# Variances of two batches computed in earlier gaps of VectorE, router scores between two transposed tiles, ten dummy products instead of eight, and eight instead of four shared tiles added ahead of the final sums

## The chip, the cores and the metric

The kernel runs on one core of a Trainium2 chip. A core has TensorE (PE: matrix products into PSUM; the weight loads before them are shown as PEld), VectorE (DVE), ScalarE (ACT), GpSimd (POOL) and SyncE (SP), which here only issues DMAs. Each engine takes its instructions strictly in the order in which they were written and waits, where it must, for marks that the other engines and the DMAs set. The metric is the time of one execution on the device, in microseconds (us).

## The reference

Four batches of 512 tokens of width 512 go through two gated residual steps. `x` is (4, 512, 512); the context is (4, 64, 128), 64 keys for each batch.

```python
def xattn(q, latent_kv, Wq, Wkv_expand, Wout):          # 16 heads of 32
    qp = q @ Wq.T
    k, v = jnp.split(latent_kv @ Wkv_expand.T, 2, axis=-1)
    scores = jnp.einsum('bhqd,bhkd->bhqk', qh, kh) / sqrt(32)
    scores = jnp.where(tril, scores, finfo.min)
    out = jnp.einsum('bhqk,bhkd->bhqd', softmax(scores), vh)
    return out @ Wout.T

def ffn(x, gate_w, w1, w2, w3, ws1, ws2, ws3):          # 8 experts, inner width 256
    scores = softmax(xf @ gate_w.T)
    weights, idx = top_k(scores, 2)
    eo = silu(xf @ w1.T) * (xf @ w3.T) @ w2.T           # per expert
    y = sum over the two chosen experts of weight * eo
    z = silu(xf @ ws1.T) * (xf @ ws3.T) @ ws2.T         # shared expert
    return y + z

x = x + tanh(g_xattn) * xattn(layernorm(x), ctx, ...)
x = x + tanh(g_ffn)   * ffn(layernorm(x), ...)
```

The layer norm has no weights: each row minus its mean, divided by sqrt(variance + 1e-5). Everything is float32.

## The kernel before

Tokens lie in tiles of 128 rows, four to a batch, sixteen in all. The kernel has three stages, and in each the order of the work on PE, DVE, ACT and POOL is the order of the Python statements (a "manual schedule"); no planner moves anything on these four engines. SP's order is by hand in the stage of the experts only.

**Attention** (`attention()`). The loop `for b in range(B)` handles the attention of batch b, and beside it the end of batch b-1 ("last"): its output projection (`project_out`, PE tile `pd`, L360), the residual sum into `xs` (L364), the second norm, and the router. For one batch:

- `score_products` (PE tile `psc`, L299) makes the scores of two of the four tiles; it is called twice.
- `largest` (DVE, L314) finds each row's maximum straight from `psc`; `exponentials` subtracts it (DVE, L319) and takes exp on ACT (L320); `softmax` sums (DVE, L325), inverts (L327) and lets POOL multiply (L328). The four tiles are p0 to p3.
- `transpose_p` turns one such tile on PE (eight transposes, tile `pp`, L335), and ACT copies them out (`prt`, L338, two copies a tile).
- `attend` multiplies with the values (PE tile `po`, L349; ACT copies `at`, L354).
- For batch b+1 the rows are turned (`turn`: PE `pt`, L190; ACT copies `xt`, L191) and projected (`project_q`: PE `pq`, L285, one chunk of 128 columns in 3.5 us; ACT copies `qt`, L289).
- `first_rows(b + 2)` norms the rows of batch b+2: `moments` (four pairs of DVE L148 and L149), `deviation` (DVE L155, square root on ACT L157, five small DVE operations L161 to L167) and `normalize` (four of DVE L177).
- For batch b-1, `second_rows_of` norms its rows (DVE L177), `turn` turns them into `x2t`, `gate` (PE `pg`, L372; ACT copy `parts`, L377) and `gate_sum` (PE `pl`, L383) make the router's scores. `choose` finds the two best experts by a chain of some thirty small DVE operations (L395 to L438) around one exp on ACT (L418); `route` and `scatter` then give each row its place (PE L445 and L448, DVE L454 to L459), and POOL writes each row twice into a table in DRAM (`xg_d`, indirect DMA, L464, eight for one batch).

exp, square root and SiLU need different function tables on ACT; a table load (ACT_TABLE_LOAD) stands ahead of the first use after another table. `table_of(AF.Exp)` is a tiny exp (L625) that brings that load forward.

The products in PSUM share a ring of four buffers (`ps_mm`: tiles `pp`, `pt`, `pq`, `pg`, `pl`, `po`, `pd`, `pz` and the shared expert's `ph`); the fifth product must wait until the first has been copied out. The last batch has no next batch to project (`more` is false), so two halves of the shared expert (`shared_pair`, PE L583, ACT SiLU L600, DVE product L601, which the code calls `gated`) fill the gaps.

Before the first score, PE makes eight dummy products `pw` (L630). From 25 us on SP writes zeros over `xg_d` (L246) and over the result table `y_d` (L250), some 41 MB, at the rate of the DMA queue; POOL's first indirect write may not go before the last zeros of `xg_d` have landed.

**Experts.** `last_routing` ends batch 3; then a loop over 32 to 39 tiles of 128 gathered rows: PE `ph` (L868) and `py` (L895), POOL adds each result row into `y_d` (L902).

**The end.** The shared expert's second product (`shared_down`, PE tile `pz`, L929, 1.72 us a tile) is still wanted for each of the sixteen tiles, and is multiplied by a gate and added on DVE. For the first `ahead` tiles (`shared_onto_attended`, L938) the sum goes onto `xs`, which needs nothing from the experts. For the others it goes onto `yk` (L1018), the experts' sums, two tiles to a buffer, which eight DMAs read back from `y_d` (L992), and only after DVE has added `xs` (`add_attended`, L999). `store` (SP, L1002) writes a finished tile out.

Of the kernel before, what the change touches and what calls it, by code (L numbers as in the profile page):

```python
# [15 lines left out]
AF = mybir.ActivationFunctionType  # L16
# [4 lines left out]
B, S, D = 4, 512, 512  # L21
# [3 lines left out]
DC = D // P  # L25
QT = S // P
# [21 lines left out]
def gated_cross_attention_moe(  # L48
# [157 lines left out]
    with ExitStack() as attn:  # L206
# [268 lines left out]
        def new_qt():  # L475
            return a2.tile([P, DC, S], F32, tag="qt", name="qt")

        def first_rows(b):
            for t in range(QT):
                moments(b, mv1[b], t)  # L480
            deviation(mv1[b], rstd1[b])()
            xn = [a4.tile([P, D], F32, tag="xn", name="xn") for t in range(QT)]
            for t in range(QT):
                normalize(xn[t], b, t, mv1[b], rstd1[b])
            return xn
# [132 lines left out]
        def attention():  # L618
            xn = [a4.tile([P, D], F32, tag="xn", name="xn") for t in range(QT)]
            nc.gpsimd.tensor_copy(ctx_sb[:, :, 1, :], ctx_sb[:, :, 0, :])  # L620
            small_one = small.tile([P, 1], F32, tag="one", name="one", bufs=1)

            def table_of(function):

                nc.scalar.activation(small_one, ones[:, 0:1], function)  # L625


            pw = ps_mm.tile([P, P], F32, tag="mm", name="pw")
            for _ in range(8):
                nc.tensor.matmul(pw, ident, ident, start=True, stop=True)  # L630
            table_of(AF.Sqrt)
            xt, qt = new_xt(), new_qt()
            mv, rstd = mv1[0], rstd1[0]
            for t in range(2):
                moments(0, mv, t)
            rest = deviation(mv, rstd, range(0, 2))
            for half in range(2):
                project_keys(half)
            rest()
            for t in range(2):  # L640
                normalize(xn[t], 0, t, mv, rstd)
            for t in range(2):
                transpose_rows(xn[t], t, xt)
            for t in range(2, QT):
                moments(0, mv, t)
            rest = deviation(mv, rstd, range(2, QT))
            project_q(xt, qt, range(DC), slice(0, 2 * P))
            rest()
            for t in range(2, QT):
                normalize(xn[t], 0, t, mv, rstd)  # L650
            for t in range(2, QT):
                transpose_rows(xn[t], t, xt)
            project_values(0)
            xn = first_rows(1)
            project_q(xt, qt, range(DC), slice(2 * P, S))
            for f, i in counts:
                nc.vector.tensor_copy(f, i)
            at = qt_next = None
            parts = iter([(c, f) for c in range(B - 1) for f in range(FC)])
            for b in range(B):  # L660
                more, last = b + 1 < B, b - 1
                prt = ab.tile([P, NPAIR, S], F32, tag="prt", name="prt")
                psc = score_products(b, 0, qt)
                if b > 1:
                    places, scatter = route(last - 1, *chosen)
                if more:
                    xt, qt_next = new_xt(), new_qt()
                    turn(xn, xt)
                if not b:
                    project_values(1)  # L670
                p0 = exponentials(*largest(psc, 0))
                p1 = exponentials(*largest(psc, 1))
                if not b:
                    nc.scalar.activation(tg_x, tg_x, AF.Tanh)
                    nc.scalar.activation(tg_f, tg_f, AF.Tanh)
                if b > 1:
                    places()
                softmax(p0)
                if b:
                    mv, rstd = new_stats()  # L680
                    project_out(last, at, 0)
                    moments(last, mv, 0)
                softmax(p1)
                if b > 1:
                    for t in range(QT):
                        scatter(t)
                if b:
                    for t in range(1, QT):
                        project_out(last, at, t)
                        moments(last, mv, t)  # L690
                    rest = deviation(mv, rstd)
                    if more:
                        table_of(AF.Exp)
                else:
                    project_q(xt, qt_next, range(2))
                psc = score_products(b, 1, qt)
                if not b:
                    transpose_p(p0, prt, 0)
                    transpose_p(p1, prt, 1)
                if b and more:  # L700
                    project_q(xt, qt_next, range(1))
                elif b:
                    gated, _ = shared_pair(*next(parts))
                    table_of(AF.Exp)
                p2 = largest(psc, 2)
                if b:
                    rest()
                p2 = exponentials(*p2)
                p3 = exponentials(*largest(psc, 3))
                if b:  # L710
                    if more:
                        project_q(xt, qt_next, range(1, 2))
                    else:
                        gated()
                    xn2 = new_rows(last)
                    second_rows_of(xn2, last, mv, rstd)
                softmax(p2)
                softmax(p3)
                if b:
                    transpose_p(p0, prt, 0)  # L720
                    transpose_p(p1, prt, 1)
                    turn(xn2, x2t[last])
                if more:
                    project_q(xt, qt_next, range(2, DC))
                    if b:
                        scored = gate(last)
                else:
                    gated, scored = shared_pair(*next(parts), lambda: gate(last))
                    gated()
                if b + 2 < B:  # L730
                    xn = first_rows(b + 2)
                if not more:
                    scores = gate_sum(scored)
                transpose_p(p2, prt, 2)
                if not b:
                    project_values(2)
                transpose_p(p3, prt, 3)
                if not b:
                    project_values(3)
                    table_of(AF.Exp)  # L740
                if b and more:
                    scores = gate_sum(scored)
                attended = []

                def attend_now():
                    attended.append(attend(b, prt))

                if b:
                    chosen = (xn2, *choose(last, scores, attend_now))
                else:  # L750
                    attend_now()
                (at,) = attended
                qt = qt_next

            scoring.close()
            attn.close()
            return at, chosen, parts
# [230 lines left out]
    with tc.manual_schedule(engines={ET.PE, ET.DVE, ET.Activation}):  # L988
        yk = []
        for i in range(0, NT, 2):  # L990
            yk.append(yp.tile([P, 2, D], F32, tag="yk", name="yk"))
            nc.sync.dma_start(  # L992
                out=yk[-1], in_=y_rows[ts(i // 2, 2 * P), :].rearrange("(t p) d -> p t d", p=P)
            )
        def add_attended(i):

            b, t = divmod(i, QT)
            y = yk[i // 2]
            nc.vector.tensor_tensor(y, y, xs[b][:, t : t + 2, :], ALU.add)  # L999

        def store(i, columns=slice(0, D)):
            nc.sync.dma_start(out=out[ts(i, P), columns], in_=yk[i // 2][:, i % 2, columns])  # L1002


        ahead = QT
        for i in range(1, ahead):
            shared_onto_attended(i)
        for i in range(0, ahead, 2):
            add_attended(i)
            store(i)  # L1010
            store(i + 1)
        for i in range(ahead, NT):
            if i % 2 == 0:
                add_attended(i)
            for c in range(0, D, D if i < NT - 1 else YH):
                columns = slice(c, D if i < NT - 1 else c + YH)
                y = yk[i // 2][:, i % 2, columns]
                nc.vector.scalar_tensor_tensor(  # L1018
                    y, shared_down(i, columns), tg_f, y, ALU.mult, ALU.add
                )  # L1020
                store(i, columns)
# [52 lines left out]
```

## Time and profile before

| | us |
|---|---|
| median of 3 runs (471.78 to 473.58) | 472.6 |
| the profiled execution | 474.84 |
| its span, first to last instruction | 473.1 |
| PE busy in the span | 456.8 |
| DVE, ACT, POOL busy | 250.1, 130.6, 179.2 |

All times of the trace are counted from the start of the span. The attention stage lasts until about 190 us, the routing of the last batch to 235, the experts from 246 to 435, the end from there on. In the trace's lines the first number is the start, the second the busy time, `x4` the number of instructions merged into the line, and the bracket at the end how long the engine had stood idle and what ended that.

### The profile page before, as it was taken

To read this page: it belongs to the slowest core of one execution; us is meant where nothing else is said; L and a number is where in the kernel's file an instruction comes from. 1 tells how busy PE (TensorE), PEld (TensorE's weight loads), DVE (VectorE), ACT (ScalarE), POOL (GpSimd) and SP (SyncE) were. 2 spreads that over 40 slices of the span, in tenths; PEclk is the share of its full clock that TensorE was granted. 3 is DMA by queue.
4 is the path that set the end of the run, shared out by engine and by line. 5 is a ranking of instruction groups with operands and counts; after the bars stand their busy time and mean duration, and the time that the engine had idled before them with its cause. 6 is when DMAs were issued, how large, how long until landed. Compare 5 with 4: busy or idle time off the path is not lost.

```text
span 473.1 us, 6677 instructions
## 1 busy us (share of the span) xinstructions
PE 456.8 (97%) x1970; PEld 234.1 (49%) x1970; DVE 250.1 (53%) x600; ACT 130.6 (28%) x244; POOL 179.2 (38%) x188
## 2 busy tenths in 40 slices
PE   7999999999999989999999999999999999999876
PEld 6775455564556555445444444444444444444333
DVE  3557788769937983557323333343333433333385
ACT  2345752573454274423011111111111111110000
POOL 3003312301480474342500656556565565655200
PEclk9999999999999999999999999999999999999979
DMA  7989999999964040899745766665666656544594
GB/s 274 310 308 384 386 386 385 387 385 386 400 259 87 1 183 2 321 417 418 283 84 123 120 106 104 102 97 90 103 98 104 99 91 102 70 52 57 155 395 184
DMA packets 70785, 98.13 MB, mean 207 GB/s; under 512 B 11728, under 2 KB 40144, under 8 KB 69584
## 3 DMA queue, kind: packets, MB, share of 16 engines
q1 hardware_dynamic: 58096, 80.01, 50.0%
q0 software_dynamic: 12352, 17.57, 20.8%
q8 instruction: 19, 0.31, 0.3%
q14 instruction: 30, 0.25, 0.2%
q10 hardware_dynamic: 288, 0.00, 0.0%
HBM read 34.84 MB, written 62.71 MB: 206 GB/s over the span
## 4 chain that ended last, share of the span: by engine, by line
PE 79%; DVE 10%; DMA 7%; ACT 2%; issue 1%; SPq 1%; another core or an unknown queue 0%; DVEq 0%
PE ph L868 23%; PE py L895 11%; PE pq L285 10%; PE pd L360 9%; PE ph L609 6%; DMA y_d<-y,meta 5%; PE pz L929 4%; PE pt L190 3%; PE ph L583 3%; PE psc L299 2%; DVE mx L314 2%; PE early L583 1%; PE pg L887 1%; PE pp L335 1%; DMA yk<-y_d 1%; DVE pr L319 1%
## 5 line engine op out<-in xcount | busy, mean ns | idle before, releaser
L902 POOL DMA_INDIRECT y_d<-y,meta x68 | 105.6, 1553 | 103.1 <-DVE y L899 60.9
L868 PE MATMUL ph<-w_all,xgt 128*128 x272 | 122.6, 593 | 0.1
L868 PEld LDWEIGHTS ph<-w_all,xgt 128*128 128x128 f32 x272 | 49.1, 190 | 49.6 <-issue 49.5
L328 POOL TENSOR_TENSOR pr<-pr,rs 128x1024 f32<-128x1024 f32 x16 | 30.2, 1902 | 111.9 <-DVE rs L327 91.2
L895 PE MATMUL py<-w_all,gt 128*128 x136 | 63.9, 592 | 0.0
L879 DVE SCALAR_TENSOR_TENSOR g<-sl,w,ph 128x256 f32<-128x256 f32 x34 | 16.3, 481 | 87.0 <-ACT sl L877 84.6
L285 PE MATMUL pq<-xt,wq_sb 128*128 128x512 f32 (+1 forms) x160 | 56.9, 511 | 0.7 <-ACT xt L191 0.7
L360 PE MATMUL pd<-wo_sb,at 128*128 128x512 f32 x128 | 56.1, 595 | 0.0
L877 ACT ACTIVATE sl<-ph 128x256 f32<-128x256 f32 x34 | 13.1, 384 | 109.0 <-PE ph L868 58.1
L895 PEld LDWEIGHTS py<-w_all,gt 128*128 128x128 f32 x136 | 25.8, 190 | 32.5 <-issue 32.5
L285 PEld LDWEIGHTS pq<-xt,wq_sb 128*128 128x128 f32 x160 | 29.7, 190 | 24.3 <-issue 20.1
L360 PEld LDWEIGHTS pd<-wo_sb,at 128*128 128x128 f32 x128 | 23.9, 190 | 29.1 <-issue 27.3
L899 DVE COPY y<-py 128x512 f32<-128x512 f32 x34 | 23.5, 692 | 27.8 <-PE py L895 27.8
L929 PE MATMUL pz<-sh,gs_sb 128*128 128x512 f32 (+1 forms) x68 | 31.0, 615 | 5.5 <-DVE yk L1018 4.6
L609 PE MATMUL ph<-x2t,sh 128*128 128x512 f32 x64 | 28.6, 596 | 0.0
L889 ACT COPY gt<-pg 128x256 f32<-128x256 f32 x34 | 12.7, 372 | 53.1 <-PE pg L887 53.1
L148 DVE BATCH_NORM_STATS2 st<-x 128x6 f32<-128x512 f32 x32 | 21.8, 680 | 7.3 <-DMA x<-in_x_dram 6.8
L929 PEld LDWEIGHTS pz<-sh,gs_sb 128*128 128x128 f32 x68 | 13.8, 207 | 22.4 <-issue 15.8
L856 DVE STREAM_TRANSPOSE xgt<-xg 128x512 f32<-128x512 f32 x34 | 23.9, 702 | 0.9 <-DMA xg<-xg_d 0.9
L320 ACT ACTIVATE pr<-pr 128x1024 f32<-128x1024 f32 x16 | 16.9, 1058 | 18.8 <-DVE pr L319 15.5
L464 POOL DMA_INDIRECT xg_d<-xn,pos x16 | 16.1, 1009 | 12.1 <-issue 10.5
L325 DVE TENSOR_REDUCE sm<-pr 128x16 f32<-128x1024 f32 x16 | 19.1, 1191 | 0.0
(167 smaller groups left out, 495.4 us busy)
## 6 DMA issues: line engine op xcount, KB each, us to landing
xg_d<-gs_sb SPq DMA_DIRECT2D x8, 4224.0 KB
xg<-xg_d SPq DMA_DIRECT2D x144, 64.0 KB
w_all<-in_w_dram SPq DMA_DIRECT2D x8, 1024.0 KB
y_d<-gs_sb SPq DMA_DIRECT2D x1, 4352.0 KB
w_all<-in_w_dram SPq DMA_DIRECT2D x8, 512.0 KB
yk<-y_d SPq DMA_DIRECT2D x8, 512.0 KB
out_dram<-yk SPq DMA_DIRECT2D x15, 256.0 KB
x<-in_x_dram SPq DMA_DIRECT2D x3, 1024.0 KB
```

The lines of the kernel that those rows point to most:

```text
L148: nc.vector.bn_stats(st, xs[b][:, t, :])
L285: nc.tensor.matmul(pq, wq_sb[:, k, ts(c, P)], xt[:, k, tokens], start=(k == 0), stop=(k == DC - 1),)
L325: nc.vector.tensor_reduce(sm, pr, AX.X, ALU.add)
L328: nc.gpsimd.tensor_tensor(pr, pr, rs.broadcast_to([P, NH, SK]), ALU.mult)
L360: nc.tensor.matmul(pd, at[:, c, ts(t, P)], wo_sb[:, c, :], start=(c == 0), stop=(c == DC - 1),)
L609: nc.tensor.matmul(ph[:, w, :], sh13[:, w, k, ts(f, P)], x2t[b][:, k, :], start=(k == 0), stop=(k == DC - 1),)
L856: nc.vector.transpose(xgt.rearrange("p c t k -> p t c k"), xg.rearrange("p t (c i) -> p t c i", c=DC))
L868: nc.tensor.matmul(ph, xgt[:, k, :], w13_all[:, ds(e, 1), :, k, :], start=(k == 0), stop=(k == DC - 1),)
L895: nc.tensor.matmul(py, gt[:, f, :], w2_all[:, ds(e, 1), f, :], start=(f == 0), stop=(f == FC - 1))
L899: nc.vector.tensor_copy(y, py)
L902: nc.gpsimd.indirect_dma_start(out=y_w[h], out_offset=IndirectOffsetOnAxis(ap=goes[j][:, h : h + 1].bitcast(I32), axis=0), in_=y[:, ts(h, ...
L929: nc.tensor.matmul(pz, gs[b][:, f, ts(t, P)], sh2[:, f, columns], start=(f == 0), stop=(f == FC - 1),)
```

## The change

Five edits, all of order but one:

1. Ten dummy products instead of eight.
2. `first_rows` is cut in two: `first_moments` (moments, the addition of epsilon and the square root) and the rest. For batch 2 the first part, followed by a return to the exp table, goes ahead of the second half of batch 0's scores, and the rest into the gap between the third and the fourth chunk of `project_q`. For batch 3 both parts go there.
3. In the last batch, the subtraction, exp and softmax of p3 go behind the transposes of p0, p1 and of the second-norm rows.
4. In batches 1 and 2, `gate_sum` goes between the transposes of p2 and p3 instead of behind both.
5. `ahead` is 8 instead of 4.

```diff
-        def first_rows(b):
+        def first_moments(b):
             for t in range(QT):
                 moments(b, mv1[b], t)
-            deviation(mv1[b], rstd1[b])()
+            return deviation(mv1[b], rstd1[b])
+
+        def first_rows(b, rest):
+            rest()
             xn = [a4.tile([P, D], F32, tag="xn", name="xn") for t in range(QT)]
...
-            for _ in range(8):
+            for _ in range(10):
                 nc.tensor.matmul(pw, ident, ident, start=True, stop=True)
...
-            xn = first_rows(1)
+            xn = first_rows(1, first_moments(1))
...
                 else:
                     project_q(xt, qt_next, range(2))
+                    first_rest = first_moments(b + 2)
+                    table_of(AF.Exp)
                 psc = score_products(b, 1, qt)
...
                 p2 = exponentials(*p2)
-                p3 = exponentials(*largest(psc, 3))
+                p3 = largest(psc, 3)
+                if more:
+                    p3 = exponentials(*p3)
...
                 softmax(p2)
-                softmax(p3)
+                if more:
+                    softmax(p3)
                 if b:
                     transpose_p(p0, prt, 0)
                     transpose_p(p1, prt, 1)
                     turn(xn2, x2t[last])
                 if more:
-                    project_q(xt, qt_next, range(2, DC))
+                    project_q(xt, qt_next, range(2, 3))
+                    if b + 2 < B:
+                        if b:
+                            first_rest = first_moments(b + 2)
+                            table_of(AF.Exp)
+                        xn = first_rows(b + 2, first_rest)
+                    project_q(xt, qt_next, range(3, DC))
                     if b:
                         scored = gate(last)
                 else:
+                    p3 = exponentials(*p3)
+                    softmax(p3)
                     gated, scored = shared_pair(*next(parts), lambda: gate(last))
                     gated()
-                if b + 2 < B:
-                    xn = first_rows(b + 2)
-                if not more:
                     scores = gate_sum(scored)
                 transpose_p(p2, prt, 2)
                 if not b:
                     project_values(2)
+                elif more:
+                    scores = gate_sum(scored)
                 transpose_p(p3, prt, 3)
                 if not b:
                     project_values(3)
-                    table_of(AF.Exp)
-                if b and more:
-                    scores = gate_sum(scored)
...
-        ahead = QT
+        ahead = 2 * QT
         for i in range(1, ahead):
             shared_onto_attended(i)
```

The instructions are the same on POOL and on SP, in the same order. PE has two products more. ACT loses no copy and no exp; one table load falls away in batch 1, where the router's exp now finds its table in place.

## The prediction

> **What bounds the kernel now.** I read the page first: engine totals, clock row. Then PE's waits, the timeline around each wait, and the end by windows.
>
> ```profile
> PE 456.8 (97%) x1970; PEld 234.1 (49%) x1970; DVE 250.1 (53%) x600; ACT 130.6 (28%) x244; POOL 179.2 (38%) x188
> ...
> PEclk9999999999999999999999999999999999999979
> ...
> PE pz L929 <- DVE yk L1018: 4.6, 1, 4.6
> PE pp L335 <- ACT prt L338: 0.9, 1, 0.9
> PE pp L335 <- DVE pr L319: 0.9, 1, 0.9
> PE pl L383 <- ACT prt L338: 0.8, 1, 0.8
> ```
>
> PE is busy for 97%, so time comes only from its few waits (total, times, longest), or from work at a lowered clock, which counts as busy: the 7 stands in the second last slice, 449 to 461 us. From 190 to 435 us PE hardly waits and nothing changes there; what PE gains before 190 arrives whole at the end.
>
> A wait before 140 us is worth nothing, though. POOL and PE in batch 2:
>
> ```profile
> 126.65 1.19 POOL L464 DMA_INDIRECT xg_d<-xn,pos  x1 [6.10 <-issue]
> 138.83 3.76 POOL L328 TENSOR_TENSOR pr<-pr,rs 128x1024 f32<-128x1024 f32 x2
> ...
> 141.52 2.22 PE L335 MATMUL pp<-ident,pr 128*128 128x128 f32 x16
> 143.57 0.96 PE L383 MATMUL pl<-part,parts 128*128 128x8 f32 x8
> 144.46 1.95 PE L349 MATMUL po<-prt,vals 64*32 64x512 f32 x32
> ```
>
> POOL's first scatter waits from 118.7 to 125.6 for the last zeros in the scatter table, written at the DMA queue's own rate whatever PE does. Eight scatters of about 1.3 us and eight small writes follow, then the products of p2 (done 140.71) and p3 (done 142.59), which PE transposes. However early PE comes, it meets these two times.
>
> Batch 3, then the end:
>
> ```profile
> 173.19 0.68 DVE L601 TENSOR_TENSOR gs_sb<-gs_sb,ph 128x512 f32<-128x512 f32 x1
> 173.93 0.66 PE L335 MATMUL pp<-ident,pr 128*128 128x128 f32 x4 [0.88 <-DVE pr L319]
> 174.33 2.03 ACT L338 COPY prt<-pp 128x512 f32<-128x512 f32 x4
> 174.95 2.12 PE L190 MATMUL pt<-ident,xn 128*128 128x128 f32 x16 [0.37 <-DVE xn L177]
> ...
> 435.88 12.26 PE L929 MATMUL pz<-sh,gs_sb 128*128 128x512 f32 x28 [0.88 <-DVE y L899]
> 452.75 16.82 PE L929 MATMUL pz<-sh,gs_sb 128*128 128x512 f32 x36 [4.61 <-DVE yk L1018]
> ...
> 444.00:452.00 8.00, 4.13 (x10) 1.52 (x8) 3.73 (x4) 0.00 (x0) 0.00 (x0) 0.98 0.89 310
> 452.00:458.00 6.00, 5.25 (x6) 2.19 (x7) 5.77 (x7) 0.00 (x0) 0.00 (x0) 0.50 1.05 400
> 458.00:462.00 4.00, 4.00 (x10) 1.86 (x9) 2.60 (x3) 0.00 (x0) 0.00 (x0) 0.95 1.05 406
> 462.00:473.10 11.10, 7.57 (x22) 3.80 (x20) 6.18 (x9) 0.00 (x0) 0.00 (x0) 0.95 0.45 170
> ```
>
> The windows' last three columns are clock, DMA share, GB/s. PE idles 4.61 us, then works at clock 0.50 (in the clock record from 451.61 to 458.44). DMA is full from 446 to 462 and half empty after: there the stores wait for PE.
>
> **Part by part.** Edit 1: sixteen passes (two per product) take 3.78 us; four more, 0.95 at most, end at 6.4 instead of 5.5, before the projected keys can start at 6.72 (their DMA). Cost 0; if that cover went, 0.95. A gain is possible: the clock is 0.5 until 11.29, and the keys' eight passes and eight transposes (3.75 and 1.54) would shrink by up to 1.9 if it rose one step earlier. 0 to -1.9, before the gate.
>
> Edit 2, batch 0: DVE is free from 39.42; four moments (0.79 apart) and the epsilon end at 42.85, so the first maximum (42.31 before) is 0.6 late. On ACT two table loads (1.28 each), the square root and the tiny exp (0.2 each) now stand ahead of p0's and p1's four copies: these start at about 44.6 instead of 42.87. Behind them waits PE: the third chunk of `pq` needs a PSUM buffer that the first copy frees, 45.2 instead of 43.98, +1.2. In return the table load at 51.65 and its square root no longer stand before p2's copies, and PE's 0.94 at 54.2 and 0.6 before `po` go. Net about -0.3 to +0.5.
>
> Here a page of the Trainium skill speaks against the edit. The row first: the load at 103.64 takes 1.28, and its exp starts at 104.94, no drain between. "ScalarE: Activation LUTs", section "What ACT_TABLE_LOAD costs", puts a switch at 1.28 plus a drain of 1.38. By the page, an estimate, the pair here would cost 2.8 more and the gate below would be missed by most of its 0.7; the sum would then be -6.3 instead of -7.0. No row here shows the drain.
>
> Edits 2 and 4, batch 1: the table load (96.78) and square root (98.07) leave the place before `prt`, so these copies start near 96.8 instead of 98.18; the norming of batch 3's rows ends near 96.8 instead of 101.2, so `choose`'s first copy no longer keeps `po`'s buffer. PE: 0.87 for p2, 0.81 for `pl`, 0.87 for p3, then two copies: `po` starts near 98.9 instead of 99.79 and runs 1.95 instead of 2.69. Gain 1.6 (0.9 to 2.1).
>
> All this meets the gate. PE would reach p2 at 141.5 less 1.3 to 4, that is 137.5 to 140.2, and waits until 140.75. From there: p2 to 141.6, `pl` to 142.4, p3 from 142.64 (POOL), first half 143.1, its copy 0.59, `po` at 143.75 instead of 144.46. **Batch 2: -0.7** (0 to -0.9; the 144.46 held `pl` behind p3). Here `choose` starts 2 us earlier, but its exp waits behind `at`'s copies, so DVE's next chain starts at 148.55 instead of 149.71.
>
> The idle time at the gate, 0.6 to 3.3, raises a clock question. The row: 4.61 idle brought clock 0.50 for 6.83. "TensorE: Matmul & The Clock Gate", "Why this matters for your kernels", allows no gap over about 3 us. By the page, an estimate, a gap of 3.3 would halve the clock and lose some 3.4; the sum would be -3.6. The nearest rows below are waits of 1.2 and 1.7, without a drop; 3.3 is the extreme, so I charge nothing.
>
> Edit 3, batch 3. PE's second half of p1 waits for the buffer of `ph`, released by L601 at 173.87: DVE stands at p3's subtraction (172.05) first. ACT's `prt` copies wait behind p3's exp (173.37 to 174.43), so the row transposes get their buffers late. After: L601 follows the second maximum, near 172.0 done; `prt` starts at 171.4 behind p2's exp; PE's transposes run 170.87 to 172.65, the rows' (norming from 172.0, 0.46 apart) to 174.45 instead of 177.07. That is 2.6, with batch 2's 0.7 in it: **-1.9** (0 if the norming stayed; -2.0 is the floor, 3.5 for 32 transposes against 5.5). Late next is p3: subtraction to 177.2, exp 178.3, sum and inverse 179.8, POOL 181.7; PE wants it at 184.3. Cover 2.6; once gone, PE waits. The edit adds no table load.
>
> Edit 5. PE runs tiles 1 to 11 without a wait, to 454.75 at 1.72 each; tiles 1 to 7 leave through DVE by 448.92. Then DVE: five sums of 1.3 (batches' `yk` in by 447.4, 448.7, 450.6, 451.9, 453.3 by the landing marks, so none waits long), tile 8 done near 456.2, and pairs at the 2.64 seen (453.27 to 455.91) to 465.0. PE waits 1.5 for tile 12's buffer, under any gap that cost clock here, and ends at 463.2. The last store takes 1.73 from issue to landing (470.12 to 471.85): 466.8 by DVE. Now the queue: 8.39 MB in all, 6.5 by 462 (310x8 + 400x6 + 406x4), 1.89 left at 406 is 4.7, with 0.6 for landing 467.4 (by marks: first eight stores landed by 462.33, 0.63 apart, eight more tiles 467.4). Before 471.85. **-4.4**: DMA is the bound, DVE 0.6 behind. Ends: -3.1 (clock drops again, below) and -5.0 (DVE's time).
>
> Sum: -0.7 -1.9 -4.4 = -7.0. The profiled 474.84 (span 473.1 and 1.74 around) becomes 467.8. That execution is 2.2 over the median, so the median goes from 472.6 to 465.6.
>
> **Rivals.** (a) Clock drops again at the end: PE's wait for tile 12 grows past what keeps the clock. Four tiles at 3.43 for 6.83 us: PE ends at 466.6, DVE 467.2, last landing 468.8: -3.1, total -5.7, 466.9. For: this is where it fell before. Against: 1.5 instead of 4.6.
> (b) Batch 3 keeps its waits, since DVE's maximum there starts 1.1 late (167.57, scores done 164.67) for a cause no row names; if norming stays where it was, -5.1, 467.5.
> (c) The second half of the end fails: store data go out behind all reads (store 0 issued 448.73, landed 457.94), and if reads slow to the 310 of the first window the end gains only 1.5: 468.5.
> (d) No gate: if POOL's wait shortens with PE, batch 1's 1.6 and some of edit 1's 1.9 count: -9, 463.6. Against: the wait is for DMA alone.
> (e) Slower: the long gap at the gate (up to 3.3) leaves PE at clock 0.50, and it does not return while PE micro-waits. Each us at half clock costs 0.5; from 14 us on it eats all 7.0, at 24 us the time is 477.6. Against: the one drop lasted 6.83, with PE busy.
> (f) The edits do not do what they say: the order of instructions shows that they do, so only the cover could hide them; then about 472.6.
>
> **The numbers.** Forecast 0.55, (a) 0.10, (b) 0.10, (c) 0.08, (d) 0.06, (e) 0.05, (f) 0.06. Under 0.5%, 2.4 us, this kernel's measurement (spread 1.8) cannot tell a change. Faster: 0.89; same 0.06; slower 0.05. The forecast alone: 464 to 467. The range takes in (a) to (d) and the runs' spread: 463.0 to 469.3.
>
> **What the profile after would show.** Right: no wait of about 4.6 at `pz`, the clock at 1.0 to the end, DMA share 1.05 until about 460, counted on the new axis; the last `po` of batch 2 near 143.7 whatever the earlier shift; the 0.88 and 0.37 in batch 3 gone. Wrong: a clock of 0.5 anywhere past 12 us; POOL's first scatter away from 126.6; `pp` of p3 in batch 3 waiting for POOL.

## The result and the profile after

The changed kernel takes 470.62 us, the median of 20 runs (468.12 to 471.85); the kernel before, run beside it, 471.78 (469.91 to 476.29, 20 runs). The ratio is 0.9966, 95% interval 0.9949 to 0.9984: 1.6 us faster (0.8 to 2.4), and not the 7.0 that were forecast. The profiled execution took 470.11, with a span of 468.4.

The page of the changed kernel, engine totals and clock row, and then PE's waits (total, times, longest), answer the lines of before:

```profile
PE 453.6 (97%) x1974; PEld 234.5 (50%) x1974; DVE 251.5 (54%) x600; ACT 130.9 (28%) x245; POOL 178.6 (38%) x188
...
PEclk9999999999997999999999999999999999999999
```

```profile
PE pp L335 <- POOL pr L328: 3.1, 1, 3.1
...
PE pq L285 <- ACT prt L338: 0.9, 1, 0.9
...
PE pz L941 <- DVE yk L1030: 0.5, 1, 0.5
```

Two things changed places. The wait of 4.6 at `pz` is down to 0.5, and the 7 in the clock row, which stood in the second last slice, has gone from there. But a wait of 3.1 for POOL, which before did not have, has come up, and the 7 now stands in the thirteenth slice, 140 to 152 us: right behind that wait.

The timeline of the changed kernel, first at the start, then at the place that the prediction calls the gate (POOL first, then PE), then batch 3 and the end:

```profile
6.49 2.16 PE L263 MATMUL pk<-ctx_sb,wkv_sb 128*128 128x256 f32 x8 [0.16 <-DMA wkv_sb<-in_wkv_dram]
...
10.58 5.63 PE L285 MATMUL pq<-xt,wq_sb 128*128 128x256 f32 x25 [1.05 <-DMA wq_sb<-in_wq_dram]
...
126.27 1.20 POOL L464 DMA_INDIRECT xg_d<-xn,pos  x1 [10.98 <-issue]
138.13 3.76 POOL L328 TENSOR_TENSOR pr<-pr,rs 128x1024 f32<-128x1024 f32 x2
...
135.96 1.07 PE L372 MATMUL pg<-x2t,gate_sb 128*32 128x512 f32 x8
140.09 1.97 PE L335 MATMUL pp<-ident,pr 128*128 128x128 f32 x8 [3.06 <-POOL pr L328]
141.85 1.71 PE L383 MATMUL pl<-part,parts 128*128 128x8 f32 x8
143.41 1.95 PE L335 MATMUL pp<-ident,pr 128*128 128x128 f32 x8
145.29 2.68 PE L349 MATMUL po<-prt,vals 64*32 64x512 f32 x32
...
150.31 4.97 PE L360 MATMUL pd<-wo_sb,at 128*128 128x512 f32 x11
...
173.14 1.91 PE L335 MATMUL pp<-ident,pr 128*128 128x128 f32 x16
...
176.69 3.60 PE L586 MATMUL ph<-rows_sb,sh 128*128 128x512 f32 x8
...
435.78 19.12 PE L941 MATMUL pz<-sh,gs_sb 128*128 128x512 f32 x44 [0.88 <-DVE y L911]
455.40 7.14 PE L941 MATMUL pz<-sh,gs_sb 128*128 128x512 f32 x20 [0.50 <-DVE yk L1030]
```

At the start everything goes as well as the prediction thought possible: the keys take 2.16 instead of 3.75, and the first `pq` comes at 10.58 instead of 12.49. At the gate PE is done with `pg` at 137.02; before was done at 141.59. So PE comes 4.6 earlier to a POOL whose first write starts at 126.27, only 0.4 earlier than before. (In both traces that write starts 1.02 behind the last landing mark of the zeros, 125.25 here and 125.63 before.) PE stands idle for 3.06, and what follows is slow: `pl` takes 1.71 where before showed 0.96, eight transposes 1.97 and 1.95 where sixteen took 2.22. The next residual product, `pd`, starts at 150.31; before had it at 148.75. PE was 4.6 us ahead of the kernel before when it reached the gate, and is 1.6 us behind it when it leaves. PE's timeline of before at the two places:

```profile
140.52 1.06 PE L372 MATMUL pg<-x2t,gate_sb 128*32 128x512 f32 x8
...
148.75 9.69 PE L360 MATMUL pd<-wo_sb,at 128*128 128x512 f32 x22
```

Batch 3 and the end come out as forecast: the transposes of batch 3 run without a wait, 3.55 from 173.14 to 176.69 (before 5.34), and `pz` runs in one stretch of 44 and, after half a microsecond, one of 20.

Windows over the end of the changed kernel (busy time of the engines; the last three columns are clock, DMA share, GB/s):

```profile
444.00:452.00 8.00, 8.00 (x20) 3.61 (x19) 5.43 (x6) 0.00 (x0) 0.00 (x0) 1.00 0.98 354
452.00:458.00 6.00, 5.50 (x13) 2.20 (x12) 5.79 (x8) 0.00 (x0) 0.00 (x0) 1.00 1.05 400
458.00:462.00 4.00, 4.00 (x14) 2.33 (x13) 3.90 (x5) 0.00 (x0) 0.00 (x0) 1.00 1.05 405
462.00:468.40 6.40, 0.55 (x3) 0.14 (x1) 1.96 (x4) 0.00 (x0) 0.00 (x0) 0.95 0.62 235
```

PE works at full clock until its last product ends at 462.5, and the queue moves 400 to 405 GB/s from 452 to 462. The last store lands at 467.09; before, 471.85.

The clock record of the two profiled executions (start, length, clock), up to the last product of PE; behind it both have 0.50 again, which costs nothing:

```
before   11.29 440.32 1.00 | 451.61  6.83 0.50 | 458.44  13.65 1.00
after     6.90 133.12 1.00 | 140.02  6.83 0.50 | 146.85 320.85 1.00
```

Both have one such drop of 6.83 us. The change took it from the end and got it back at the gate.

### The profile page after: what moved, and what is told of

Same layout as the page of the kernel before. It is cut to its first block, busy times and chain, and to the rows that moved or that the text cites. A ratio compares the mean times of both kernels' runs of the same rounds, so it can differ in the third digit from the quotient of the medians.

```text
span 468.4 us, 6683 instructions
## 1 busy us (share of the span) xinstructions
PE 453.6 (97%) x1974; PEld 234.5 (50%) x1974; DVE 251.5 (54%) x600; ACT 130.9 (28%) x245; POOL 178.6 (38%) x188
## 4 chain that ended last, share of the span: by engine, by line
PE 65%; SPq 15%; DMA 9%; issue 3%; DVE 3%; POOL 2%; ACT 0%; DVEq 0%; ACTq 0%; POOLq 0%
PE ph L880 25%; SPq L246 15%; PE py L907 12%; PE ph L612 6%; PE pd L360 6%; PE ph L586 4%; DMA xg_d<-gs_sb 4%; PE pz L941 3%; DMA wo_sb<-in_wo_dram 2%; DMA x<-in_x_dram 2%; POOL xg_d L464 2%; DVE yk L1011 2%; PE pg L899 2%; PE early L586 1%; PE pp L335 1%
## 5 line engine op out<-in xcount | busy, mean ns | idle before, releaser
L941 PE MATMUL pz<-sh,gs_sb 128*128 128x512 f32 (+1 forms) x68 | 28.1, 570 | 1.4 <-DVE y L911 0.9
L941 PEld LDWEIGHTS pz<-sh,gs_sb 128*128 128x128 f32 x68 | 12.7, 190 | 16.6 <-issue 15.1
L335 PE MATMUL pp<-ident,pr 128*128 128x128 f32 x128 | 17.8, 293 | 3.1 <-POOL pr L328 3.1
```

Of the source, the lines that this page charges most:

```text
L941: nc.tensor.matmul(pz, gs[b][:, f, ts(t, P)], sh2[:, f, columns], start=(f == 0), stop=(f == FC - 1),)
```

## The experiments

The expectations of a run name theories; the letters belong to that run, and each is told with it. In short, what is in question: did edit 5 fail to bring its 4.4 in an ordinary execution, or do edits 1 to 4 lose most of it at the gate? Ratios are against the kernel before on the same chip; in parentheses is the 95% interval.

**The kernel before, once more.** No edit.

> The kernel before, unchanged, for its spread from run to run. Theory A (the clock's steps are not tied to the kernel, so PE's 4.61 us at the end costs a clock drop in some executions only): the executions differ in mean clock, and those with less clock lost are about 3 us shorter; the median lies near 471.8, and a profile without the drop has a span near 470 with PE's last products at full clock. Theory B (each execution pays the drop; the first profile was long for another reason): clock and time hang together no more than by chance, and a new profile shows clock 0.50 behind the wait for the final sums again.

472.16 us (470.51 to 473.93, 12 runs), ratio 0.9998 (0.9979 to 1.0017). Neither theory came as it stands. Clock and time do hang together: six runs list a mean clock of 0.989 to 0.992 and take 472.2 to 473.9, six list 0.996 and take 470.5 to 472.2. But no run lists more than 0.996, and the new profile has a drop behind the wait for the final sums again, half as long. What matters is this profile, a second execution of before, here the timeline of PE:

```profile
170.98 1.91 PE L335 MATMUL pp<-ident,pr 128*128 128x128 f32 x16
173.12 2.12 PE L190 MATMUL pt<-ident,xn 128*128 128x128 f32 x16 [0.24 <-ACT prt L338]
175.08 3.69 PE L583 MATMUL ph<-rows_sb,sh 128*128 128x512 f32 x8
...
434.03 12.26 PE L929 MATMUL pz<-sh,gs_sb 128*128 128x512 f32 x28 [0.88 <-DVE y L899]
449.93 15.71 PE L929 MATMUL pz<-sh,gs_sb 128*128 128x512 f32 x36 [3.65 <-DVE yk L1018]
```

The stretch of batch 3 that edit 3 is about takes 4.10 here, not 5.34: the waits of 0.88 and 0.37 are absent but for 0.24. At the end the wait is 3.65, not 4.61, and the clock is at 0.50 for 3.41 (450.38 to 453.80), not 6.83; from the start of `pz` to the end of the span it is 35.2 instead of 37.2. The profile on which the prediction was built was thus of an execution 3.1 us over the median of the 20 runs; of the 3.9 between its time and this one's (474.84 and 470.90), 3.2 lie in the two places that edits 3 and 5 touch.

**Edit 5 alone.** On the kernel before:

```diff
-        ahead = QT
+        ahead = 2 * QT
```

> The kernel before with edit 5 alone (eight tiles added ahead). Theory A: 4.4 us less than an execution with the drop at the end, but only 1.5 less than one without, so 1.5 to 2.5 us (0.995 to 0.997 of before) in the median. Theory B (the end gains its 4.4 in every execution and edits 1 to 4 lose some 3 of it): 4.4 us, 0.991.

467.97 us (467.50 to 468.74, 6 runs), ratio 0.9914 (0.9891 to 0.9938): 4.1 us faster, close to the prediction's -4.4 and to theory B. One edit out of five brings 2.5 us more than all five. PE's timeline at its gate:

```profile
138.39 1.06 PE L372 MATMUL pg<-x2t,gate_sb 128*32 128x512 f32 x8
139.94 1.09 PE L335 MATMUL pp<-ident,pr 128*128 128x128 f32 x8 [0.48 <-POOL pr L328]
141.80 1.09 PE L335 MATMUL pp<-ident,pr 128*128 128x128 f32 x8 [0.77 <-POOL pr L328]
```

Here PE arrives at 139.45, waits 0.48 and 0.77, and the clock record has 1.00 from 5.79 to 463.18 without a break.

**Edits 1 to 4 without edit 5.** On the changed kernel:

```diff
-        ahead = 2 * QT
+        ahead = QT
```

> The changed kernel with four shared tiles, not eight, added ahead of the sums: edits 1 to 4 without edit 5. Theory A (the clock's drop at batch 2's gate takes what the start and batches 0 and 1 give, and edit 3 is worth 0.5): the end costs again about what it does in the kernel before, so the ratio to the kernel before is 0.999 to 1.005; in the profile PE waits about 3 for POOL before the products of p2 in batch 2 and works at clock 0.50 for 3.4 or 6.8 right behind. Rival (the prediction's own terms, -0.7 and -1.9, hold): -2.6, ratio 0.9945.

473.53 us (470.17 to 475.32, 12 runs), ratio 1.0012 (0.9990 to 1.0033). What was to bring -2.6 brings nothing. The timeline of PE:

```profile
136.26 1.06 PE L372 MATMUL pg<-x2t,gate_sb 128*32 128x512 f32 x8
140.07 1.10 PE L335 MATMUL pp<-ident,pr 128*128 128x128 f32 x8 [2.75 <-POOL pr L328]
141.00 1.68 PE L383 MATMUL pl<-part,parts 128*128 128x8 f32 x8
```

The wait is 2.75, and the clock falls at 141.03, for 6.83; it falls once more at the end, at 451.64, for 6.83, as before's did. These two runs settle the first half of the answer: the end's term holds, and edits 1 to 4 together bring nothing.

**Filling the gap.** On the changed kernel, twelve dummy products (nothing uses them) between `pg` and the first transposes of p2 in batch 2:

```diff
+                if b == 2:
+                    pw = ps_mm.tile([P, P], F32, tag="mm", name="pw")
+                    for _ in range(12):
+                        nc.tensor.matmul(pw, ident, ident, start=True, stop=True)
```

> The changed kernel with twelve dummy products of 128x128 on PE behind the router's products of batch 2, where PE stands idle for 3.06 us; they take 2.6 us of that idle time. Theory A (the idle time takes the clock to 0.50 for 6.83 us, and this eats the gain): clock 1.0 through batch 2, the products with the values of batch 2 start near 143.1 instead of 145.29, batch 3's output projection near 147.4 instead of 150.31, about 2.9 us less than the changed kernel, 0.990 of before. Rival (the low clock costs nothing, since POOL and DVE set the pace there): same time as the changed kernel, 0.9966.

466.70 us (466.51 to 467.63, 6 runs), ratio 0.9886 (0.9863 to 0.9909). PE's timeline:

```profile
135.97 1.06 PE L372 MATMUL pg<-x2t,gate_sb 128*32 128x512 f32 x8
136.97 2.94 PE L750 MATMUL pw<-ident 128*128 128x128 f32 x24
140.96 1.09 PE L335 MATMUL pp<-ident,pr 128*128 128x128 f32 x8 [1.05 <-POOL pr L328]
141.89 0.96 PE L383 MATMUL pl<-part,parts 128*128 128x8 f32 x8
...
148.45 10.12 PE L360 MATMUL pd<-wo_sb,at 128*128 128x512 f32 x23
```

Work that nobody needs makes the kernel 3.8 us faster (0.0080 of the ratio, give or take 0.0029 by the two intervals). POOL is no earlier here (its first write starts at 127.13, 0.9 later than in the changed kernel); what is different is the clock, 1.00 all the way from 5.83 to 463.22. From the transposes of p2 to `pd` it is 7.49 here and 10.22 in the changed kernel: the drop costs 2.7 in the profiled execution. The kernel before needs 7.23 for it.

**Filling a third of it, and the changed kernel beside it.** The same edit with 4 products instead of 12; and no edit.

> The changed kernel with four dummy products (8 passes, 0.98, nothing uses them) ahead of the products of p2 in batch 2, where twelve were tried: some 2.0 of the idle time are left. Theory A (the clock falls only when a window of 3.4 has less than about 1 of work; 1.83 idle had no drop, 2.75 had one): no drop in most executions, median within 1 of the version with twelve, ratio 0.987 to 0.991. Rival (2.0 idle are too long already): the drop stays and the median is that of the changed kernel, 0.995 to 0.998.

> The changed kernel unaltered, on one chip with the version of it that has four dummy products at batch 2's gate, for a comparison on the same chip and for a second profile of the gate. Theory A (the idle time at the gate is near 3 in every execution, since ten dummy products always bring the clock up early): ratio 0.995 to 0.998, and clock 0.50 for 3.4 or 6.8 behind the gate in this profile too. Rival (the drop belonged to the profiled execution, the usual one has none): no drop in this profile, and the loss stands elsewhere.

The changed kernel: 470.32 us (468.66 to 473.44, 12 runs), ratio 0.9966 (0.9942 to 0.9990), the same as in the first measurement, and its profile has the same picture, a wait of 3.23 and the clock at 0.50 from 140.44, for 6.83. With four dummy products: 468.62 (467.06 to 471.14, 8 runs), ratio 0.9932 (0.9905 to 0.9959), between the two ranges expected and outside both. Without dummy products, with four and with twelve products it is 0.9966, 0.9932, 0.9886. With four, the drop seems to come in some executions only: three of the eight list a mean clock of 0.989 and take 470.6 to 471.1, the other five list 0.996 to 0.998 and take 467.1 to 469.1. The profiled one was among the three: POOL was late in it (first write 127.26), so that 2.95 of waiting were left in spite of the products. For the others only the mean clock is known, and it also counts the low clock behind PE's last product (in this profile 0.50 from 465.99 on), so it doesn't show by itself where the clock was lost.

**Eight dummy products at the start, not ten.** On the changed kernel:

```diff
-            for _ in range(10):
+            for _ in range(8):
```

> The changed kernel with eight dummy products at the start, as in the kernel before, not ten. Theory A (the clock's steps have a phase of their own, which two more products don't set, and the gate takes what the start gives): 0.995 to 0.998, like the changed kernel (0.9966), and the same gate with its drop. Rival (the two products are what brought the early rise of the clock and with it the long idle time at the gate): the first projected q at 12.5 instead of 10.6, the idle time at the gate near 1.2, no drop behind it, ratio 0.990 to 0.992.

470.28 us (466.04 to 471.59, 12 runs), ratio 0.9940 (0.9912 to 0.9968): between the two ranges expected again. It looks like a mixture: four runs list a mean clock of 0.998 to 1.000 and take 466.0 to 467.9, eight list 0.986 to 0.994 and take 469.4 to 471.6. The profile is of one of the four, PE's timeline:

```profile
6.53 3.75 PE L263 MATMUL pk<-ctx_sb,wkv_sb 128*128 128x256 f32 x8 [1.05 <-DMA wkv_sb<-in_wkv_dram]
...
137.61 1.06 PE L372 MATMUL pg<-x2t,gate_sb 128*32 128x512 f32 x8
140.50 1.09 PE L335 MATMUL pp<-ident,pr 128*128 128x128 f32 x8 [1.83 <-POOL pr L328]
```

The clock rose late (10.82), the keys took 3.75, PE came to the gate at 138.67, 1.65 later than in the changed kernel, waited 1.83 and kept its clock: here a late start goes with a fast execution. Whether the clock rose early in the other eight was not seen, since a run shows its mean clock only.

**Edit 3 alone.** On the kernel before, in the last batch:

```diff
-                p3 = exponentials(*largest(psc, 3))
+                p3 = largest(psc, 3)
+                if more:
+                    p3 = exponentials(*p3)
...
-                softmax(p3)
+                if more:
+                    softmax(p3)
...
                 else:
+                    p3 = exponentials(*p3)
+                    softmax(p3)
```

> The kernel before with edit 3 alone (the scores of the experts between the turned tiles). Theory A (the late maximum of the profiled execution was of that execution only): from the first `pp` to the last row transpose of batch 3 3.55 instead of 4.1, -0.5, ratio 0.9985 to 1.0. Rival (the prediction's term): -1.9, ratio 0.996.

471.64 us (469.32 to 472.65, 12 runs), ratio 0.9979 (0.9959 to 1.0000): 1.0 us faster, with 0 to 1.9 in the interval, which does not exclude either of the two numbers expected. In the profile the stretch takes 3.49 (170.73 to 174.22), against 4.10 in the second profile of before. The edit does what it says, but there is less for it to take away than the 5.34 of the first profile.

**Taking the gate away.** On the changed kernel, batch 2's eight writes go behind POOL's products of p2 and p3:

```diff
-                if b > 1:
+                if b > 1 and not more:
                     for t in range(QT):
                         scatter(t)
...
                 if more:
                     softmax(p3)
+                if b > 1 and more:
+                    for t in range(QT):
+                        scatter(t)
```

> The changed kernel with batch 2's eight scatters issued by POOL behind its products of p2 and p3 instead of ahead of them, so these no longer wait for the zeros. Theory A: PE does not wait in batch 2, transposes p2 right behind the router's products at about 137, the values' products start near 139.9 instead of 145.29; this arrives at the experts, 5 us less than the changed kernel, 0.986 of before. Rival (a later fixed time takes it back: the shared weights' load, or POOL's scatters of batch 3 started late): 1 to 2 us less than the changed kernel, or none, with a new wait in batch 3 or ahead of the experts.

464.24 us (463.87 to 464.55, 5 runs), ratio 0.9833 (0.9808 to 0.9858): 7.9 us faster than before and the best version here; 5 us less than the changed kernel were expected, and it is 6.3. The timeline, POOL and then PE:

```profile
127.68 3.76 POOL L328 TENSOR_TENSOR pr<-pr,rs 128x1024 f32<-128x1024 f32 x2 [11.43 <-ACT prt L338]
131.87 1.19 POOL L464 DMA_INDIRECT xg_d<-xn,pos  x1 [0.29 <-POOL xn L462]
...
135.87 1.07 PE L372 MATMUL pg<-x2t,gate_sb 128*32 128x512 f32 x8
136.87 1.09 PE L335 MATMUL pp<-ident,pr 128*128 128x128 f32 x8
...
139.91 1.95 PE L349 MATMUL po<-prt,vals 64*32 64x512 f32 x32 [0.24 <-ACT prt L338]
...
144.21 13.98 PE L360 MATMUL pd<-wo_sb,at 128*128 128x512 f32 x32
```

POOL's products no longer stand behind the wait for the zeros; PE goes from `pg` to the transposes without a wait, and `pd` starts at 144.21, 4.5 earlier than before and 6.1 earlier than in the changed kernel. The writes into the table start 5.6 later than in the changed kernel, and PE has no longer wait for it anywhere (its longest past the start is 0.9). The runs lie within 0.7 us; those of the changed kernel spread over 3.7 to 4.8.

**Edit 5 and the late writes, without edits 1 to 4.** The same late writes on the kernel before, with `ahead = 2 * QT`:

> The kernel before with eight tiles added ahead of the sums, and with batch 2's eight scatters behind POOL's products of p2 and p3; none of the edits 1 to 4. Theory A (what edits 1 to 4 give ahead of the gate counts whole once the gate is gone): they are worth 1.5 to 3, so this kernel stands that much above the version with the edits and the late scatters (ratio 0.9833): 0.987 to 0.9895. Rival (edits 1 to 4 are worth nothing, with a gate or without): 0.983 to 0.985.

468.01 us (466.40 to 469.14, 6 runs), ratio 0.9896 (0.9866 to 0.9926). Against 0.9833 this prices edits 1 to 4 where no gate stands in their way: 0.0063, or 3.0 us, give or take 1.8 by the two intervals, which were taken on two chips. Late writes beside edit 5 (0.9896) can't be told from edit 5 alone (0.9914) by their intervals. So no cost of the gate to the kernel before shows beyond these intervals; it became a cost when PE came early.

## Why the prediction was wrong

**The step that failed** is the one on the idle time at the gate: "3.3 is the extreme, so I charge nothing". The idle time was 3.06, inside the 0.6 to 3.3 that the prediction itself had worked out, and the clock fell to 0.50 for 6.83. Batch 2's -0.7 became +1.6 in the profiled execution (`pd` at 150.31 instead of 148.05), and that is the size of the 2.3 between the 467.8 forecast for the profiled time and the 470.11 that came (what else differs, 0.3 each way, cancels). The prediction had named a clock of 0.5 past 12 us as a sign that it was wrong. That the gap is the cause, and not another part of the edits, is shown by the run that fills it. The reason given for charging nothing, that the nearest waits in the profile of before, 1.2 and 1.7, showed no drop, does not hold. PE's timeline of before has these two waits, and the longest one behind them in the stage of attention:

```profile
1.70 3.78 PE L630 MATMUL pw<-ident 128*128 128x128 f32 x16 [1.70 <-POOL ident masks.py:199]
6.72 3.75 PE L263 MATMUL pk<-ctx_sb,wkv_sb 128*128 128x256 f32 x8 [1.24 <-DMA wkv_sb<-in_wkv_dram]
...
54.22 0.66 PE L335 MATMUL pp<-ident,pr 128*128 128x128 f32 x4 [0.94 <-ACT prt L338]
```

The first two end ahead of 11.29, where the clock record first has 1.00: the clock had not yet risen, so they can't show whether it would have fallen. At the raised clock the longest wait without a drop was 0.94, and the next row was the 4.61 with one, only 1.3 away from the extreme. Between the two no row of before shows anything, so the term needed a price in the range, and got none. Rival (e) named this mechanism, but asked what would eat all of the 7.0, not what one drop of the length seen would cost. A drop of that length, 6.83, came here too and cost 2.7.

The section of the Trainium skill weighed there ("TensorE: Matmul & The Clock Gate", "Why this matters for your kernels") allows no gap over about 3 us, and the gap of 3.06 did bring the drop; in this case gaps of 2.75 and 2.95 did too (last section). The estimate by it was a sum of -3.6; the two profiled executions differ by 4.7, the runs by 1.6.

**What went right.** Edit 5: -4.4 forecast, -4.6 between the two profiles from the start of `pz` to the end of the span (37.2 to 32.6), -4.1 in the runs of the edit alone. DMA was forecast as the bound: the queue moves 400 to 405 GB/s, the last store takes 2.9 from issue (464.2) to landing where it took 1.73 before, and the last landing, forecast for 467.4, came at 467.09. DVE has hardly any slack either (busy for 5.79 of the 6.00 us from 452 to 458). Rivals (a) and (c) did not happen. Batch 1: `psc` starts at 98.45, before at 102.40; without the 1.9 of the start and 0.6 from batch 0 that is 1.4, forecast 1.6. Batch 0: the third chunk of `pq` waits 0.91 for the copy that now stands behind two table loads (1.2 forecast), and the net, read at the next `psc` (55.57 instead of 58.09, less the 1.9), is -0.6 (forecast -0.3 to +0.5). The timeline of ACT there:

```profile
39.00 1.28 ACT L157 ACT_TABLE_LOAD   x1
40.88 0.20 ACT L157 ACTIVATE sd<-ve 128x4 f32<-128x4 f32 x1 [0.59 <-DVE ve L155]
41.09 1.28 ACT L628 ACT_TABLE_LOAD   x1
42.38 0.20 ACT L628 ACTIVATE one<-ones 128x1 f32<-128x1 f32 x1
```

The second load ends at 42.37, and the next instruction starts at 42.38: no drain stands between them, as the row of before said, and not as "ScalarE: Activation LUTs", "What ACT_TABLE_LOAD costs", has it (1.38 more).

**What was mis-sized.** Edit 3's -1.9 holds between the two profiled executions (5.34 to 3.55), but it is -1.0 in the runs of the edit alone and 0.6 by its profile against the second profile of before. Rival (b) had the reason in hand: DVE's maximum began 1.1 late, for no cause that a row named. In the second profile it is not late. What made it late in the one execution stays open. A smaller slip: POOL's wait for the zeros in before starts at 120.55 by its row (6.10 ahead of 126.65), not at 118.7; no term rests on it.

**Carrying the sum over.** The prediction saw that its profile stood 2.2 over the median and took the whole -7.0 off the median. But part of the 2.2 was in the very terms: batch 3 was 1.2 longer, the end 2.0 longer than in the second profile. In the runs the terms are -4.1 (edit 5) and -1.0 (edit 3), against -4.4 and -1.9.

**What stays open.** The parts don't quite add up: edit 5 alone and edits 1 to 4 alone give 0.9914 and 1.0012, together 0.9926, and the changed kernel 0.9966. The difference, 0.0040, is slightly more than the three intervals allow (0.0036, taken as independent). From these, edits 1, 2 and 4 with the gate cost 1.6 (no edit 5) to 3.5 (from the whole), where -0.7 was forecast; either number can be off by 1.4 or more. Rival (d), 463.6 without a gate, did not come by itself, since POOL's wait is for DMA alone (its first write is at 126.27 although PE is 4.6 earlier), as was argued against it; the version that takes the gate away comes to 464.24.

## What to carry to other kernels

An engine that arrives early at a wait it cannot shorten gains nothing, and on PE the longer idle time can cost more than was gained, because the clock falls. Price the drop, with the length and the loss that the trace shows, as soon as the worked-out gap is longer than the longest one known to be harmless; and count as harmless only a gap at which the clock was up and could have fallen. Take away the gate (here an order of POOL's instructions) before speeding up what runs into it. And read a gain off two executions, since the one profiled may be long just where the change works.

## What the runs showed that was not expected

**How little idle time is enough.** The clock's steps lie 3.41 apart within an execution (133.12 is 39 of them, 440.32 is 129), so the stretch of 3.41 that ends at a drop can be looked at. Windows over two of them, 3.40 long, the first in the changed kernel, with the one behind it:

```profile
136.60:140.00 3.40, 0.42 (x4) 0.00 (x0) 0.00 (x0) 0.64 (x2) 3.15 (x11) 1.00 0.93 262
140.00:143.40 3.40, 3.31 (x16) 3.31 (x17) 0.00 (x0) 1.17 (x2) 1.90 (x2) 0.50 0.67 159
```

and the one with the gate in the kernel with eight dummy products:

```profile
137.10:140.50 3.40, 1.57 (x10) 0.16 (x9) 0.00 (x0) 1.17 (x2) 3.15 (x11) 1.00 0.67 227
```

| kernel and place | idle | PE busy in the 3.40 | then |
|---|---|---|---|
| before, end | 4.61 | 0.00 | 0.50 for 6.83 |
| changed, second profile, gate | 3.23 | 0.17 | 0.50 for 6.83 |
| changed, gate | 3.06 | 0.42 | 0.50 for 6.83 |
| before, second profile, end | 3.65 | 0.47 | 0.50 for 3.41 |
| four products in the gap | 2.95 | 0.65 | 0.50 for 6.83 |
| edits 1 to 4, gate | 2.75 | 0.93 | 0.50 for 6.83 |
| eight at the start, gate | 1.83 | 1.57 | 1.00 |

PE need not be idle for the whole stretch: 0.93 us of work in it did not save the clock, 1.57 did. But the kind of work differs: the 0.93 and the 0.65 are transposes alone, the 1.57 products of `pq` and `pg`. The length of the drops points the same way. Behind the end of the second profile PE is busy with `pz` for all 3.40 of the first low stretch, and the clock comes back after 3.41. Behind the gate it is busy for 3.31 to 3.41 in four profiles, with transposes (`pp`) and the router's narrow products (`pl`), and the clock comes back only after 6.83. That would fit transposes that count for less than products; no run here varies it, so it stays open. The section "What's actually happening" of "TensorE: Matmul & The Clock Gate" speaks of at least one idle window of about 3.4 us; by these rows a window with 0.47 us of products in it, or with 0.93 us of transposes, can count as one.

**When the clock rises at the start.** With eight dummy products it rose at 11.29, 10.06, 10.82, 10.19, 5.79 and 5.32 in the six executions profiled, with ten at 6.90, 7.32, 7.91, 5.83, 6.98 and 5.19. The two products, 0.95 us at most, did not make the early rise possible, but in these records it came each time with them. The traces show where the difference lies. In all twelve executions the stretch of 3.41 that ends at the rise holds 3.09 us of PE work or more; in the four late ones the stretch ahead of it holds 2.2 to 2.4, because PE stands idle for 1.05 to 1.24 between the eight products and the keys. In the two early ones with eight most or all of that idle time lies behind the rise. With ten that idle time is 0.16 to 0.69. The early rise is worth 1.9 at the first `pq` (10.58 against 12.49).
